# A macaron transformer block on one core: the first feed-forward takes both blocks for each group of weights, and the stages between run in an order written by hand

## The chip, the cores and the metric

The kernel runs on one core of one Trainium2 chip. The metric is the device time of one execution in microseconds. Three runs of the kernel before took 3497.04, 3499.12 and 3503.48 us, so the median is 3499.12. The engines have short names in all that follows: PE (TensorE, matmul), PEld (its weight loads), DVE (VectorE), ACT (ScalarE), POOL (GpSimd) and SP (SyncE, which here only issues DMA transfers). Each engine has its own queue and works through it in order.

## The reference

The input x is 4 batches of 1024 rows of 512 floats. What is computed is a feed-forward, an attention and the same feed-forward again, each added to x:

```
x = x + 0.5 * ffn(layernorm(x))
x = x + attn(layernorm(x))       # 32 heads of 16, 8 of keys and values, rotary positions
x = x + 0.5 * ffn(layernorm(x))
```

The feed-forward's weights are quantised first, which is part of the work: each weight is rounded to bfloat16, and in groups of 64 it becomes -scale, 0 or scale, where scale is the group's mean magnitude (0 where twice the magnitude does not exceed the scale). Then gate and up are two products of x with 2048 columns each, h = silu(gate) * up, h is divided by its root mean square per row, and a last product brings it back to 512 columns. In attention the largest score of each row is subtracted before the exponential, and the sums of the exponentials divide at the end.

## The kernel before

Rows of x are kept in tiles of 128 rows by 512 (`x_b_i`), and a *block* is four of them, 512 rows, so a batch has two blocks and there are eight in all. The hidden 2048 columns are cut into 16 *groups* of 128 (`hc`). Values that need more than one pass of TensorE's fast 32-bit format are split in two (`high` and `low`, `xT` and `xL`), and each product is made with both.

The program is a row of stages. First comes a feed-forward over the two blocks of batch 0 ("0a" in tile names), which also quantises the weights. Then, for each batch, come the *stage between* (`attention_input_output`, L520), a feed-forward over three blocks (some of old batches that are finished, some of coming ones), and the *heads* of that batch. A last stage between and a last feed-forward of two blocks end it.

*The first feed-forward* (L963 to L971, `FeedForward.chunks` at L392). For block 0, `prepare` calls `ternary_weights` (L105) for each group: three loads of 256 KB into `w`, a cast to 16 bits on ACT (L120), a reduction by groups on DVE (L122), the scales spread out on ACT (`wide`, L128), eight DVE instructions of 128x1536 for magnitude, comparison, sign and rounding (L137 to L148), twelve transposes on PE, and three copies back on ACT, of which two, the gate and up weights, are also stored in DRAM (`d_guT`, L158) and widened to 32 bits (L102). The group's products follow: 16 matmuls for gate and up (L289), Silu on ACT (L299), the product h on DVE (L301), its square and the running sum on POOL (L309, L313), high on ACT (L315), low on DVE (L317), and, one group later, eight matmuls of the projection (L329). For block 1 the gate and up weights come back from DRAM, and ten of its groups also turn one tile of the attention weights (`attention_weights`, L164) and store it in `d_w`. In this feed-forward the order of the instructions on each engine is chosen by the framework's planner, from costs and dependencies. The later feed-forwards are in program order (`tc.manual_schedule`, L383).

*The stage between* (L520) normalises eight tiles of the new batch, turns them (L210), multiplies them with the weights of queries, keys and values (L633), adds biases (L647 to L649), rotates (two products on POOL, L659 and L660, a product and a sum on DVE, L661 and L662), turns the result (L671, L672), splits it and stores it in `d_q` and `d_k` (L679, L684). In between it projects the old batch's heads (`put`, L734), adds the result to x (L745 on DVE, L746 on POOL), and normalises the first block of the next feed-forward (`follow`). With `new` absent, in the last one, only the projection and `follow` are left. The planner orders this stage too.

*The heads* go through 128 steps per batch (`run`, L847). A step makes scores (L862), exponentials (L873) and weighted sums (L883) of one part of one of eight key groups, and beside it the row maxima of groups to come. When a group's maxima are complete, they are turned, stored in `d_m` and read back as rows (`mT`, L803 and L816), with transfers issued by POOL. After every second group the sums are fetched back, inverted, stored, and read as `rec`; POOL multiplies `aT` with it (L716):

```
if self.after and n in (self.when + 7, self.when + 12):
    self.after.pop(0)()          # first invert, then multiply
```

`self.when` is the step at which the pair of groups ended (32, 64, 96). The transfers that load a place in the ring of weights, queries and keys (`Places`) are issued by SP when the place is free; in steps 100 and after, these are the weights of the next stage between (`p_in`, `p_out`).

## Time and profile before

| | |
|---|---|
| median of three runs | 3499.12 us |
| profiled execution, its own time | 3501.13 us |
| its span, first to last instruction | 3499.3 us |
| granted PE clock, mean | 0.978 |
| PE, DVE, ACT, POOL busy | 95%, 62%, 51%, 26% |
| first feed-forward, to the last projection of block 1 | 0 to 295.8 us |
| stages between, batches 0 to 3, and the last | 62.6, 87.7, 87.1, 88.7, 49.9 us |
| heads of batches 0 to 3 | 345.7, 340.1, 341.4, 329.2 us |

A line of a group of instructions reads: line in the kernel, engine, operation, output and inputs, their shapes, how many; then the busy time and the mean duration of one in ns; then how long the engine was idle just before them, and what ended that. A line of a timeline begins with the start and the duration in us, and the idle time before it stands in brackets. A line of busy times by stretch has each engine's busy time with the number of its instructions, then the clock granted to PE, the DMA engines' busy share, and GB/s. "SPq" and "POOLq" are transfers issued by that engine.

### The profile page before, as it was taken

Reading aid. Unit: us, or ns where it says so; the run is one execution under the profiler, and the core shown is the slowest. Engines: PE = TensorE matmul, PEld = TensorE weight load, DVE = VectorE, ACT = ScalarE, POOL = GpSimd, SP = SyncE. Lnnn points to the kernel's source line nnn. Section 1 sums busy time; section 2 is a strip of 40 time slices with the busy share of each in tenths; the row PEclk is TensorE's granted clock in tenths of the full one; section 3 lists DMA queues with packets and bytes.
Section 4 is the critical chain, followed back from the end, with each engine's and each line's share of the span. In section 5 each row is a group of like instructions: output and inputs, shape, how many; then the busy total and the mean of one; then the engine's idle time right before and its main releaser. Section 6 shows DMA issues by size and latency. Waiting matters only on the chain. (4 is left out here: it accounts for less than half of the span.)

```text
span 3499.3 us, 57264 instructions
## 1 busy us (share of the span) xinstructions
PE 3321.5 (95%) x22744; PEld 2151.5 (61%) x22744; DVE 2170.9 (62%) x3663; ACT 1769.6 (51%) x2372; POOL 912.0 (26%) x880
## 2 busy tenths in 40 slices
PE   5699999999989999999899999999899999999899
PEld 3577677644448777544467777444487776444587
DVE  8945566677725666677535666777346666775243
ACT  5642333377852333587733333788613334787343
POOL 2344333300014333101123333000133432010144
PEclk9999999999999999999999999999999999999999
DMA  5233322122223133132223222223231221232011
GB/s 183 78 93 102 98 59 76 51 82 89 90 74 107 55 90 100 40 108 94 81 59 101 82 69 64 66 88 103 66 103 57 87 90 56 90 98 71 27 49 55
DMA packets 211115, 282.66 MB, mean 81 GB/s; under 512 B 25760, under 2 KB 155808, under 8 KB 210848
## 3 DMA queue, kind: packets, MB, share of 16 engines
q1 hardware_dynamic: 205728, 276.89, 25.6%
q8 instruction: 179, 2.93, 0.3%
q0 software_dynamic: 5120, 2.11, 0.3%
q14 instruction: 88, 0.72, 0.1%
HBM read 220.20 MB, written 58.72 MB: 80 GB/s over the span
## 5 line engine op out<-in xcount | busy, mean ns | idle before, releaser
L774 DVE TENSOR_REDUCE pm<-sm 128x1 f32<-128x512 f32 x2048 | 1285.1, 685 | 378.6 <-PE sm L765 375.3
L873 ACT ACTIVATE e<-s 128x1024 f32<-128x1024 f32 x1024 | 996.8, 1022 | 345.4 <-PE s L862 342.8
L765 PE MATMUL sm<-p_m,p_m 32*128 32x512 f32 x4096 | 769.8, 440 | 23.6 <-DVE h L301 10.0
L289 PE MATMUL gu<-xT,guT 128*128 128x512 f32 x1792 | 706.1, 394 | 4.9 <-ACT guT L102 4.6
L289 PE MATMUL gu<-xL,guT 128*128 128x512 f32 x1792 | 700.7, 391 | 0.0
L862 PE MATMUL s<-p_s,p_s 32*128 32x512 f32 x4096 | 679.6, 440 | 0.5 <-DMA p_s<-d_k 0.4
L862 PEld LDWEIGHTS s<-p_s,p_s 32*128 32x128 f32 x4096 | 315.7, 186 | 457.6 <-ACT e L873 435.4
L883 PE MATMUL o<-e,vs 128*32 128x512 f32 x4096 | 557.0, 616 | 2.8 <-ACT e L873 2.8
L862 PE MATMUL s<-mT,ones_r 2*128 2x512 f32 x2048 | 415.8, 400 | 25.3 <-DMA mT<-d_m 25.2
L765 PEld LDWEIGHTS sm<-p_m,p_m 32*128 32x128 f32 x4096 | 355.4, 185 | 118.2 <-DVE h L301 66.8
L309 POOL TENSOR_TENSOR sq<-h 128x512 f32<-128x512 f32 x210 | 218.4, 1040 | 704.4 <-DVE h L301 704.1
L289 PEld LDWEIGHTS gu<-xT,guT 128*128 128x128 f32 x1792 | 337.6, 188 | 80.0 <-ACT guT L102 5.5
L289 PEld LDWEIGHTS gu<-xL,guT 128*128 128x128 f32 x1792 | 337.6, 188 | 69.0
L301 DVE TENSOR_TENSOR h<-sg,gu 128x512 f32<-128x512 f32 x224 | 153.9, 687 | 361.2 <-PE gu L289 358.4
L299 ACT ACTIVATE sg<-gu 128x512 f32<-128x512 f32 x224 | 134.2, 599 | 481.4 <-PE gu L289 481.4
L329 PE MATMUL po<-w_pT,high 128*128 128x512 f32 x896 | 372.0, 415 | 0.0
L329 PE MATMUL po<-w_pT,low 128*128 128x512 f32 x896 | 351.6, 392 | 0.1
L315 ACT CAST high<-h 128x512 fp32r<-128x512 f32 x224 | 139.0, 620 | 346.0 <-DVE h L301 341.8
L102 ACT CAST guT<-g 128x512 fp32r<-128x512 bf16 x448 | 274.7, 613 | 15.1 <-DMA g<-d_guT 8.1
L313 POOL TENSOR_TENSOR acc<-acc,sq 128x512 f32<-128x512 f32 x205 | 275.8, 1346 | 16.1
L862 PEld LDWEIGHTS s<-mT,ones_r 2*128 2x128 f32 x2048 | 199.3, 187 | 55.7 <-DMA mT<-d_m 28.3
L329 PEld LDWEIGHTS po<-w_pT,high 128*128 128x128 f32 x896 | 168.9, 189 | 97.5 <-issue 66.0
(134 smaller groups left out, 3032.4 us busy)
## 6 DMA issues: line engine op xcount, KB each, us to landing
g<-d_guT SPq DMA_DIRECT2D x448, 128.0 KB
p_m<-d_k SPq DMA_DIRECT2D x64, 512.0 KB
p_s<-d_k SPq DMA_DIRECT2D x64, 512.0 KB
p_m<-d_q SPq DMA_DIRECT2D x32, 512.0 KB
p_s<-d_q SPq DMA_DIRECT2D x32, 512.0 KB
d_o<-oT SPq DMA_DIRECT2D x64, 256.0 KB
x<-in_L_attn_x_dram SPq DMA_DIRECT2D x32, 256.0 KB
w<-in_L_ffn_w_gate_up_dram SPq DMA_DIRECT2D x32, 256.0 KB
```

The lines of the kernel that those rows point to most:

```text
L102: nc.scalar.copy(w, t)
L289: nc.tensor.matmul(pg, lhsT=self.weights[k, hc][part][:, c, :], rhs=xp[:, c, :], start=(c == 0 and low == 0), stop=(c == DC - 1 and low == 1),
L301: nc.vector.tensor_tensor(h, sg, gu[1], ALU.mult)
L309: nc.gpsimd.tensor_tensor(sq, h, h, ALU.mult)
L313: nc.gpsimd.tensor_tensor(acc, acc, sq, ALU.add)
L315: nc.scalar.copy(high, h)
L329: nc.tensor.matmul(self.pos[k][i], lhsT=h[:, i * P : (i + 1) * P], rhs=w_pT[hc], start=(hc == 0 and n == 0), stop=(hc == HC - 1 and n == 1),)
L765: nc.tensor.matmul(s, lhsT=q[at, i * P : (i + 1) * P], rhs=k[part][at, half * 512 : (half + 1) * 512], start=(part == 0), stop=(part == 1),)
L774: nc.vector.tensor_reduce(pm[:, i, j, half : half + 1], s, AX.X, ALU.max)
L862: nc.tensor.matmul(s[:, e, :], lhsT=k[part][at, keys] if part < 2 else ones_r[at, :], rhs=(q if part < 2 else self.mrows[g])[at, queries], ...
L873: nc.scalar.activation(w, s, AF.Exp, scale=1.0 / HD**0.5)
L883: nc.tensor.matmul(o[j * SLOT : (j + 1) * SLOT, :], lhsT=vs[:, kc, g, :], rhs=es[j // 2][:, j % 2, :], start=(kc == 0), stop=(kc == NT - 1),)
```

## The change

The first feed-forward is a class of its own, `First`. It takes the blocks of batch 0 together: group `i` of the loop quantises ahead (loads of group i+4, cast of i+3, scales and doubled magnitudes of i+2, signs and rounding of i+1), turns the weights of group i, and makes gate and up of block 1 for group i-2 and of block 0 for group i. Block 0 is projected within the loop (group i-2); block 1's hidden values are all kept, and projected after it (`projection`). Twice the magnitude is made by ACT (one activation, Abs with scale 2) instead of two DVE instructions. The weights turned go straight to 32 bits on ACT, and POOL makes the 16-bit copy that is stored. Block 0's low halves are made by POOL; block 1's squares by ACT. The attention weights are turned in groups 5 to 14. The first group is done by thirds of its columns, and only four tiles of x are loaded ahead of the first weights. All is in program order.

The stages between are in program order too, as `input_output` and `output`. The gate weights of the next feed-forward are fetched at their head and widened at their end. In `output` the four tiles of the next block are projected first and normalised together; before, statistics, turns and projections took turns. In the heads the multiplication comes at `self.when + 15`. Memory is laid out anew (x in tagged slots, `vs` in the ring's pool). The mathematics is the same.

The core of the diff:

```diff
+    class First(FeedForward):
+        def groups(self):
...
+            with tc.tile_pool(name="f0a", bufs=1) as wp, tc.tile_pool(name="wstage", bufs=1) as stage:
+                self.wp, self.stage = wp, stage
+                with tc.manual_schedule():
+                    self.begin_groups()
+                    for i in range(HC + 2):
+                        self.group(i)
+                    self.end(0, self.factors(0))
+        def projection(self):
+            with tc.manual_schedule():
+                for c in range(2):
+                    self.split(c)
+                    self.parts[1, c][1]()
+                for c in range(HC):
+                    if c + 2 < HC:
+                        self.split(c + 2)
+                    self.project(1, c, self.parts[1, c][0], [0, 1])
+                    self.project(1, c, self.parts[1, c][0], [2, 3])
+                    if c + 2 < HC:
+                        self.parts[1, c + 2][1]()
+                    if 6 <= c < 10:
+                        load_x(2, c - 6)
+                    if c == HC - 2:
+                        half = self.factors(1)
+                self.end(1, half)
...
+        def double(self, hc, some=ALL):
+            if hc < HC:
+                if hc not in self.twice:
+                    self.twice[hc] = self.sixteen("twice", hc, 2)
+                for a, z in some:
+                    at = slice(a * P, z * P)
+                    nc.scalar.activation(self.twice[hc][:, at], self.wb[hc][:, at], AF.Abs, scale=2.0)
...
+                wide, mask, wb, q = (
+                    t[hc][:, at] for t in (self.wide, self.twice, self.wb, self.q)
+                )
+                nc.vector.tensor_tensor(mask, mask, wide, ALU.is_gt)
+                nc.vector.tensor_scalar(q.bitcast(bits), wb.bitcast(bits), 0x8000, None, ALU.bitwise_and)
+                nc.vector.tensor_tensor(
+                    q.bitcast(bits), q.bitcast(bits), wide.bitcast(bits), ALU.bitwise_or
+                )
+        def quantize(self, hc, some=ALL):
+            for a, z in some if hc < HC else ():
+                at = slice(a * P, z * P)
+                mask, wb, q = (t[hc][:, at] for t in (self.twice, self.wb, self.q))
+                nc.vector.tensor_tensor(q, q, wb, ALU.subtract)
+                nc.vector.tensor_tensor(q, q, wb, ALU.add)
+                nc.vector.tensor_tensor(q, q, mask, ALU.mult)
+        def transpose(self, hc, part):
+            pt = self.ps.tile([P, DC, P], BF16, tag="gu", name=f"pw_{hc}_{part}")
+            for c in range(DC):
+                at = (part * DC + c) * P
+                nc.tensor.transpose(pt[:, c, :], self.q[hc][:, at : at + P], ident16)
+            if part == 2:
+                nc.scalar.copy(w_pT[hc].rearrange("p (c k) -> p c k", k=P), pt)
+                return
+            name = f"guT_{hc}_{part}"
+            w = (widened.tile if part else self.stage.tile)(
+                [P, DC, P], F32R, tag="guT", name=name, bufs=3
+            )
+            nc.scalar.copy(w, pt)
+            w16 = narrow_tile(f"g16_{hc}_{part}")
+            nc.gpsimd.tensor_copy(w16, w.bitcast(F32))
+            nc.sync.dma_start(d_guT[hc, part], w16.rearrange("p c k -> p (c k)"))
+            for k in range(2):
+                self.weights.setdefault((k, hc), []).append(w)
...
+        def halves(self, k, hc, engine):
+            h = self.units[k, hc]
+            high, low = (
+                self.keep.tile([P, 512], F32R, tag=n, name=f"{n}_0a_{k}_{hc}", bufs=self.LAG + 1)
+                for n in ("high", "low")
+            )
+            nc.scalar.copy(high, h)
+            self.parts[k, hc] = (high, low), lambda: engine.tensor_tensor(
+                low, h, high.bitcast(F32), ALU.subtract
+            )
+        def tally(self, k, hc, square):
+            h = self.units.pop((k, hc))
+            if hc == 0:
+                acc = self.keep.tile([P, 512], F32, tag="acc", name=f"acc_0a_{k}", bufs=1)
+                self.accs[k] = [acc]
+                square(acc, h)
+            else:
+                acc = self.accs[k][0]
+                sq = self.keep.tile([P, 512], F32, tag="sq", name=f"sq_0a_{k}_{hc}")
+                square(sq, h)
+                nc.gpsimd.tensor_tensor(acc, acc, sq, ALU.add)
+        def split(self, hc):
+            self.halves(1, hc, nc.vector)
+            self.tally(1, hc, nc.scalar.square)
+        def begin_groups(self):
+            thirds = [((a, a + 4),) for a in (0, 4, 8)]
+            for i in range(4):
+                load_x(0, i)
+            self.load(0)
+            for i in range(4, NT):
+                load_x(0, i)
+            for third in thirds:
+                self.cast(0, third)
+            self.load(1)
+            self.double(0, thirds[0])
+            scales = normal_scales(self.tiles(0), "0a_0")
+            for widen in self.scales(0, thirds[0]):
+                widen()
+            turns = list(self.normalize(0, range(4), self.wp, self.ps, "gu", 4, scales))
+            self.signs(0, thirds[0])
+            self.quantize(0, thirds[0])
+            for turn in turns:
+                turn()
...
+        def group(self, i):
+            self.finish(0, i - 1)
+            if 2 <= i:
+                for some in ([0, 1], [2, 3]):
+                    self.project(0, i - 2, self.parts[0, i - 2][0], some)
+            if 1 <= i <= HC:
+                self.halves(0, i - 1, nc.gpsimd)
+                self.parts[0, i - 1][1]()
+                self.tally(0, i - 1, lambda dst, h: nc.gpsimd.tensor_tensor(dst, h, h, ALU.mult))
+            if 1 <= i < HC:
+                for part in range(3):
+                    self.transpose(i, part)
+            steps = self.scales(i + 2)
+            if i < 2:
+                if i > 0:
+                    self.start(0, i)
+                some = [2 * i, 2 * i + 1]
+                scales = normal_scales(self.tiles(1, some), f"0a_1_{i}")
+                self.signs(i + 1)
+                for turn in self.normalize(1, some, self.wp, self.ps, "gu", 4, scales):
+                    turn()
+            else:
+                self.start(1, i - 2)
+                self.signs(i + 1)
+            if 5 <= i < 15:
+                turn = self.attention_weights(i - 5)
+            self.cast(i + 3)
+            self.load(i + 4)
+            self.double(i + 2)
+            for widen in steps:
+                widen()
+            if i >= 2:
+                self.finish(1, i - 2)
+            if 2 <= i < HC:
+                self.start(0, i)
+            self.quantize(i + 1)
+            if 5 <= i < 15:
+                turn()
+            if 2 <= i < 2 + NT:
+                load_x(1, i - 2)
...
+    def output(old, put, then, wp, ps):
+        for i in range(6):
+            put(i, range(DC - 1))
+        while old.after:
+            old.after.pop(0)()
+        for i in range(4):
+            put(i, range(DC - 1, DC))
+        scales = normal_scales(then.tiles(0), "last")
+        for i in range(4, 6):
+            put(i, range(DC - 1, DC))
+        put(6, range(DC))
+        turns = list(then.normalize(0, range(4), wp, ps, "pt", 4, scales, 2))
+        turns[0]()
+        turns[1]()
+        put(7, range(DC))
+        turns[2]()
+        turns[3]()
+    def input_output(new, old, put, then, wp, ps):
+        turn = None
+        for n in range(NT + 2):
+            if n == 0:
+                new.normalize(0, wp, new.scales(0))
+            if 1 <= n <= NT:
+                new.project(n - 1, ps)
+            if n >= 2:
+                new.rotate(n - 2)
+            scales = new.scales(n + 1) if n + 1 < NT else None
+            after = normal_scales(then.tiles(0, [n - 5]), f"f_{new.b}_{n}") if 5 <= n < 9 else None
+            if n >= 2:
+                new.rotated_sum(n - 2)
+            if scales is not None:
+                new.normalize(n + 1, wp, scales)
+            behind, turn = turn, None
+            if after is not None:
+                (turn,) = then.normalize(0, [n - 5], wp, ps, "pt", 2, after)
+            if behind is not None:
+                behind()
+            if put is not None:
+                for i in {3: (0, 1), 4: (2,), 5: (3,), 8: (4,), 9: (5,)}.get(n, ()):
+                    put(i, range(DC))
+            if n < NT:
+                new.turn_in(n, wp, ps)
+            if n >= 2:
+                new.turn(n - 2, wp, ps)
+            if put is not None and 1 <= n < 3:
+                old.after.pop(0)()
+        places.done(("in", new.b))
+        places.load(("m", new.b, 0))
+        if put is not None:
+            for i in (6, 7):
+                put(i, range(DC))
...
-                if self.after and n in (self.when + 7, self.when + 12):
+                if self.after and n in (self.when + 7, self.when + 15):
```

## The prediction

> **What bounds the kernel now.** The page says TensorE (PE), busy 95%, so I looked for where PE is not busy. First the busy time by stretch, cut at the stage borders that PE's timeline shows: to the first gate matmul, block 0 of the first feed-forward, block 1, the stage between for batch 0, the same for batch 1, and the last one.
>
> ```profile
> PE 3321.5 (95%) x22744; PEld 2151.5 (61%) x22744; DVE 2170.9 (62%) x3663; ACT 1769.6 (51%) x2372; POOL 912.0 (26%) x880
> ```
> ```profile
> core 0: us, PE busy (x) PEld busy (x) DVE busy (x) ACT busy (x) POOL busy (x), PEclk, DMA share, GB/s
> 0.00:34.50 34.50, 5.92 (x28) 4.06 (x28) 25.94 (x50) 12.61 (x14) 4.80 (x14) 1.00 0.80 271
> 34.50:198.00 163.50, 117.57 (x572) 87.70 (x573) 149.38 (x181) 100.38 (x143) 58.38 (x29) 0.93 0.28 88
> 198.00:295.80 97.80, 97.45 (x460) 80.50 (x459) 36.47 (x55) 44.03 (x75) 46.14 (x38) 0.99 0.31 94
> 295.80:358.40 62.60, 55.38 (x280) 47.49 (x279) 44.43 (x97) 11.64 (x26) 22.98 (x24) 0.93 0.45 136
> 1027.60:1115.30 87.70, 81.99 (x412) 71.42 (x409) 46.95 (x96) 13.17 (x29) 32.41 (x30) 0.96 0.36 99
> 3264.50:3314.40 49.90, 35.68 (x149) 29.59 (x146) 13.96 (x28) 2.93 (x5) 13.29 (x12) 0.86 0.12 33
> ```
> Until 198 us PE idles 74 us while VectorE (DVE), which quantises, is busy 91% of block 0; block 1 then has PE busy throughout and DVE 37%. The batch stages idle 6 to 7 us each, the last one 14.
>
> Next the groups of instructions of the first 200 us, and one of the page:
> ```profile
> L309 POOL TENSOR_TENSOR sq_0a<-h_0a 128x512 f32<-128x512 f32 x15 | 33.0, 2199 | 97.5 <-DVE h_0a L301 97.4
> L122 DVE TENSOR_REDUCE wmean<-wb 128x24 f32<-128x1536 bf16 x16 | 27.9, 1742 | 1.2 <-ACT wb L120 1.2
> L313 POOL TENSOR_TENSOR acc_0a<-acc_0a,sq_0a 128x512 f32<-128x512 f32 x15 | 26.8, 1785 | 1.2
> L120 ACT CAST wb<-w 128x1536 bf16<-128x1536 f32 x16 | 23.6, 1473 | 8.2 <-DVE wq L147 7.0 <-DMA w<-in_L_ffn_w_proj_dram 1.2
> L144 DVE TENSOR_TENSOR wq<-wq,wide 128x1536 uint16<-128x1536 uint16 x16 | 18.1, 1134 | 0.3
> ```
> ```profile
> L309 POOL TENSOR_TENSOR sq<-h 128x512 f32<-128x512 f32 x210 | 218.4, 1040 | 704.4 <-DVE h L301 704.1
> ```
> The same square takes GpSimd (POOL) 1.04 us, and 2.20 beside the quantising. Last, three timelines (POOL, DVE, PE) near the end of the heads of batch 0, and the chain that ended last:
> ```profile
> 977.63 2.34 POOL L716 TENSOR_TENSOR aT<-aT,rec 128x1024 f32<-128x1024 f32 x1 [53.15 <-DMA rec<-d_r]
> 979.91 0.58 POOL L803 DMA_DIRECT2D d_m<-mrow  x1
> ```
> ```profile
> 968.51 0.28 DVE L801 CAST mrow<-pmT 64x128 fp32r<-64x128 f32 x1 [1.90 <-PE pmT L799]
> ```
> ```profile
> 984.16 1.27 PE L862 MATMUL s<-mT,ones_r 2*128 2x512 f32 x2 [7.76 <-DMA mT<-d_m]
> ```
> ```profile
> 2610.29 17.23 DMA p_m<-d_k
> ...
> 3275.52 6.75 DMA rec<-d_r
> 3282.34 2.34 POOL aT L716
> ...
> 3325.34 1.81 PE po L329 x8
> 3327.16 3.63 PE gu L289 x16
> ```
> The maxima were ready at 968.79, but their store stood behind the multiply on POOL's queue, which waited for rec until 977.6. PE lost 7.76 us there, and 8.78 and 8.67 at 1733 and 2482; at 3221 the chain shows 1.84.
>
> **The change, part by part.** Profiled execution: 3501.13 us, span 3499.3; median 3499.12, so 2 above it.
>
> *Before the third group.* w_0 now follows 4 x loads, not 20, so PE's first gate matmul comes near 17 instead of 34.5. DVE sets what follows: up to group 2's transposes it quantises three groups, 7.0 us each once starts overlap (1.74 reduce, 0.17 scale, is_gt 0.95, sign bits 0.55, or 0.95, three of 0.95, less about 0.08 of overlap each), normalises and splits 8 x tiles (0.67+0.18+0.55+0.68, 1.8 spaced), and 1.3 more: 21+14.5+1.3 = 37. From its first x at 3.4 that is 40; I add 8 for hand-overs to ACT and POOL in the thirds (0.5 to 1.0 each). Group 2 begins at 48 (42 to 54).
>
> *Groups 2 to 15.* PE: 8 projections 1.81, 12 transposes 0.84, two passes of 16 gate and up matmuls 7.26: 9.9, and 0.4 in the ten groups that turn attention weights. DVE: 7.0 and two products of 0.69, 8.3; |2w| (0.78+0.55) and low (0.99) leave it, waits behind POOL (wscale 0.51 on average, 0.17 alone) add about 1. ACT: cast 1.47, wide 1.47, Abs about 1.47 by L120's shape, three weight copies 0.6, two Silu 0.6, high 0.62: 8.0, with the attention copy 8.6. So none passes PE by its sum, but the queues' order does: SP's stores of d_guT now wait for POOL's two casts to 16 bits, and the load of wa stands behind them, with its transposes at the end of the same group on PE. POOL begins when high is there (1.6): low 1.3, square 2.0, add 1.5 (between 1.04 or 1.28 alone and the loaded rows), two casts 0.9 each, which no row shows: bounded by 0.5 (half of vs's memset, 0.95 for twice the elements) and 2.2 (the loaded square), nearer the lower as they have one input. That ends at 8.2; 0.6 for the issue and 2.6 to land (x_0_0: issued 0.75, read 3.39) give 11.4, transposes 0.4: 11.8 a group. Queued behind it: w's load, which then lands 4 us before its cast, and on PE the next projections. Ten at 11.8 and four at 10.2: 159 (143 if PE alone binds, 189 at 13.5).
>
> Abs beside Silu: no row has it. ACT_TABLE_LOAD is 1.283, and copies and Silu alternate in block 0 with none between; a bound is 0 to two per group, which the 11.8 mostly covers. I take 0. The Trainium skill ("ScalarE: Activation LUTs", Table sets) says that abs is filler in every set, which also makes 0; no run shows it yet.
>
> *Groups 16, 17 and the end of block 0.* Two of 5.44: 10.9. Then factors, power 1.03 on POOL, four updates 2.73, and block 1's first low 0.68 stand on PE's path: 5.4.
>
> *Block 1's projections.* 16 x 1.81 = 29, with 1 for the squares, which go through one buffer (ACT 0.6, POOL add 1.3, so near 2.0 a step against 1.81, with a lead of two): 30 (29 to 35). Its last projection ends at 48+159+10.9+5.4+30 = 253 instead of 295.8: 42 saved (12 to 57).
>
> *Stage between, batch 0.* Before: 62.6. PE's sum is 50.9 (eight tiles of pq 3.45, pkv 1.73 and 0.97 of transposes, four turns of 0.43). In fixed order the updates of block 1 (1.5 past PE's end), statistics, power, rows and turn stand ahead of the first projection: 5.2, where before the turn was made inside the feed-forward, and p_in, now loaded under the projections, cost 2.46. At the end the last rotation (adds 0.9, POOL 2.0, sum 0.8, lows ahead of it 1.2) stays bare. 64.5: 2 lost (-3 to +6).
>
> *Stages for batches 1 to 3.* PE needs 78.6 (the 50.9 and eight pa of 3.45); with start 1.5, bare copies and the last rotation about 84 against 87.7. But the first maxima need p_m, which lands 23 us after the last turn (17.23 of it the transfer). Two projections follow that turn now, not three: 3.45 of this cover goes, and where PE waited 0.7 to 0.9 it will wait near 4. So 0.6 each, 2 in all (-8 to +8).
>
> *Heads.* The multiply moves three steps (7.5 us) back, from step 108 to 111, the maxima's store and load (steps 109, 110) now precede it. Both pieces, 1.8 and up to 4 to land, run within the burst of p_in loads (rec took 8.8): mT is there near 976 to 979, wanted at 976. 6.3 of each 8.4 goes, and 1.5 at 3221: 20 saved (12 to 27). Its rec transfer is issued later too, but SP, in order, came to it at 968.7 behind the p_in loads anyway, and nothing waits for that product before the heads end. The other two multiplies of a batch meet no want of mT.
>
> *Costed at nothing.* The gate weights' fetches at the head of each batch stage: six issues of some 0.4 on SP, idle there, behind the last den transfer; if it were not, den would be late and with it aT. x loads moved into the groups (256 KB each in eight): DMA's share is 0.28 in block 0, and they are last on SP in their group. vs's memset, 0.95 on POOL, lies beside the end of block 0.
>
> *Last stage.* The aT multiply ends at 3284.7 as now. Before, 29.7 us follow it, PE taking statistics, turns and whole projections in turn. After: four last pieces 3.5, the last add on POOL 3291.6, statistics 0.9, power 1.0, rows, turns, with put(7) between them: gate at 3302. 12 saved (8 to 14).
>
> Sum: 42-2+2+20+12 = 74, so 3501-74 = 3427.
>
> The Trainium skill ("GPSIMD Engine Reference", Engine selection) speaks against part of this: it puts two-input elementwise work on VectorE, as GpSimd is about twice as slow. The trace agrees (square 1.04 to 2.20, DVE's low 0.99). By that rule low stays on DVE, the chain on POOL is 1.3 shorter and the ten groups save 13 us, 3414; by my rows DVE has the room and it costs the 13.
>
> **The rivals.**
> 1. *PE binds the groups*: POOL keeps near its unloaded 1.04 and 1.28, so wa is in time. 143 for 159: 3411. For it: DVE idles within a group; against it: the loaded rows.
> 2. *The queues bind harder*: POOL at its loaded rows throughout, 13.5 a group. 189: 3457. For it: 2.20 and 1.79; against it: DVE's share falls to 70%.
> 3. *The heads keep their stall*, since d_m and mT go through the burst anyway: 3447. For it: DMA share 0.9 there; against it: 8 KB pieces.
> 4. *Slower: the casts on POOL.* At c us each the ten groups take 10.0+2c and the other four 6.2+2c once POOL binds, 28c-34 above my 159; the 74 are spent at c = 3.9, beyond it the kernel is slower, 3519 at 4.5. For it: no such cast is in the trace; against it: 3.9 is 1.8 times POOL's longest 512-element row, the loaded 2.20.
>
> **How the numbers follow.** Mine 0.52, rivals 0.16, 0.15, 0.11 and 0.05; 0.01 that all gains end within 7 us, 0.2%, which is about what a measurement here can tell from no change. Faster 0.94, same 0.01, slower 0.05. The range goes from rival 1 with 27 in the heads and 14 in the last stage, 3402, to rival 2 with 8 lost in the batch stages instead of 2 saved, 3467; outside lie rival 4 and combinations of the ends, under 2 in 10.
>
> **What would show it.** Right: last projection of block 1 near 253; PE in groups waiting for wa's DMA; no wait over 3 us on mT; p_m's wait near 4 after each batch stage; the last stage near 37 us. Wrong: a period above 13, table loads in each group, or a heads stall that stays.

## The result, and the profile after

The changed kernel takes 3518.01 us (median of four runs) beside 3501.27 for the kernel before on the same chip: a ratio of 1.0048, 95% interval 1.0031 to 1.0066. It is slower by half a per cent, where 3427 was predicted. The profiled execution took 3512.53 us with a span of 3510.8, 11.4 more than that of before (3510.75 against 3499.34). The page gives it the same busy share as before, and PE's clock is 0.973 on the mean, before 0.978:

```profile
PE 3329.0 (95%) x22736; PEld 2154.4 (61%) x22736; DVE 2169.1 (62%) x3626; ACT 1762.8 (50%) x2346; POOL 931.6 (27%) x908
```

So the page as a whole tells nothing; the stages do. Busy times of the changed kernel by stretch: the first two groups, the loop of groups, block 1's projections, the stages between of batches 0 and 1, and the last one.

```profile
core 0: us, PE busy (x) PEld busy (x) DVE busy (x) ACT busy (x) POOL busy (x), PEclk, DMA share, GB/s
18.30:61.90 43.60, 21.72 (x76) 15.28 (x76) 30.38 (x51) 22.37 (x25) 7.27 (x8) 0.59 0.23 73
61.90:235.10 173.20, 156.43 (x816) 125.91 (x816) 143.05 (x139) 104.70 (x139) 94.07 (x77) 0.99 0.40 122
235.10:268.50 33.40, 32.02 (x136) 25.81 (x136) 19.54 (x23) 15.32 (x26) 19.46 (x16) 0.95 0.28 104
268.50:339.60 71.10, 56.41 (x280) 47.34 (x280) 49.01 (x109) 13.04 (x30) 25.87 (x27) 0.94 0.28 78
1005.00:1102.10 97.10, 83.86 (x409) 71.47 (x409) 49.11 (x105) 14.53 (x32) 35.34 (x33) 0.96 0.31 85
3277.70:3325.50 47.80, 34.47 (x149) 28.85 (x145) 14.32 (x26) 3.41 (x7) 13.68 (x10) 0.86 0.14 35
```

The stage of batch 1 is 97.1 us where it was 87.7, with PE idle 13 us in it instead of 6. Cut the same way on PE's timeline, the kernels of this study that bear on these stages stand side by side (us; the names are those of the experiments below):

| | before | after | b15 | a_old | a_rec | a_cover | a_both | a_rot | a_best |
|---|---|---|---|---|---|---|---|---|---|
| first feed-forward | 295.8 | 268.5 | 296.4 | 270.6 | 271.8 | 268.2 | 269.9 | 270.8 | 251.9 |
| stage between, batch 0 | 62.6 | 71.1 | 61.7 | 61.3 | 69.9 | 71.1 | 69.7 | 68.5 | 60.0 |
| the same, batches 1 to 3, sum | 263.5 | 290.0 | 262.5 | 262.7 | 268.6 | 293.4 | 283.7 | 264.1 | 265.5 |
| feed-forwards behind these three, sum | 963.2 | 988.0 | 972.3 | 961.1 | 988.1 | 977.1 | 964.4 | 972.4 | 963.2 |
| heads, sum of four | 1356.3 | 1335.3 | 1330.9 | 1331.5 | 1337.5 | 1335.3 | 1336.4 | 1331.4 | 1333.8 |
| last stage | 49.6 | 47.7 | 50.5 | 51.3 | 48.5 | 48.0 | 48.3 | 47.8 | 40.5 |

From before to after: 27.3 and 21.0 gained in the first feed-forward and the heads, 1.9 in the last stage; 8.5, 26.5 and 24.8 lost in the stages between and in the feed-forwards that follow them. The feed-forward of batch 0 adds 1.8. PE's waits, in total, times and longest, name the places. Before:

```profile
PE s L862 <- DMA mT<-d_m: 25.2, 3, 8.8
PE pa L734 <- POOL aT L716: 4.4, 1, 4.4
PE sm L765 <- DMA p_m<-d_k: 2.4, 3, 0.9
```

After:

```profile
PE pa L1008 <- POOL aT L990: 23.4, 4, 6.2
PE sm L1037 <- ACT sg L221: 15.5, 3, 5.8
PE pxn L136 <- DVE xn L125: 7.0, 2, 6.7
PE s L1134 <- DMA mT<-d_m: 6.7, 4, 2.8
```

The wait for `mT` went, as meant. In its place stand 23 us for `aT`, the product with `rec` (18 of them in the three stages, 5 in the last one, where before had 4.4), and 15.5 in front of the first maxima (`sm`). For the latter the trace names ACT's Silu, which was long done; it is the transfer of `p_m`, as experiment a_cover shows.

### The profile page after: what moved, and what is told of

It is laid out like the page before. It is cut to its first block, busy times and chain, and to the rows that moved or that the text cites. A ratio compares the mean times of both kernels' runs of the same rounds, so it can differ in the third digit from the quotient of the medians.

```text
span 3510.8 us, 57082 instructions
## 1 busy us (share of the span) xinstructions
PE 3329.0 (95%) x22736; PEld 2154.4 (61%) x22736; DVE 2169.1 (62%) x3626; ACT 1762.8 (50%) x2346; POOL 931.6 (27%) x908
## 4 chain that ended last, share of the span: by engine, by line
PE 79%; DVE 6%; DMA 5%; issue 5%; POOL 3%; ACT 2%; SPq 0%; POOLq 0%; DVEq 0%; ACTq 0%
PE gu L211 21%; PE s L1134 16%; PE o L1155 13%; PE po L251 11%; PE sm L1037 7%; PE pq L908 3%; PE pa L1008 2%; DMA g<-d_guT 2%; DVE pm L1046 1%; PE pkv L908 1%; PE gu_0a L532 1%; DVE x L286 1%; DMA p_s<-d_k 1%; PE pxn L136 1%; DMA rec<-d_r 1%
## 5 line engine op out<-in xcount | busy, mean ns | idle before, releaser
L1037 PE MATMUL sm<-p_m,p_m 32*128 32x512 f32 x4096 | 773.6, 441 | 36.3 <-ACT sg L221 15.5
```

Of the source, the lines that this page charges most:

```text
L1037: nc.tensor.matmul(s, lhsT=q[at, i * P : (i + 1) * P], rhs=k[part][at, half * 512 : (half + 1) * 512], start=(part == 0), stop=(part == 1),)
```

## The experiments

Each ratio is to the kernel before, run on the same chip. "Against after" is the difference of the ratios times 3500 us; one such difference is uncertain by about 8 us, so small effects are read in the traces too.

**Which part gains and which loses.** b15 is the kernel before with one edit:

```diff
-                if self.after and n in (self.when + 7, self.when + 12):
+                if self.after and n in (self.when + 7, self.when + 15):
```

> The kernel before with the heads part of the change alone: the multiply moves from step 7+5 to step 7+8 behind the end of a pair of head groups, all else as before. Theory (the heads part is a gain by itself, and the batch stages lose time for reasons of their own): PE's waits on mT near 984, 1733 and 2482 us (7.8, 8.8, 8.7) shrink to 2 or less, the three stages behind the heads stay at 87 to 89 us, and the kernel comes to 3477 to 3483, ratio to before 0.993 to 0.995. Rival A (the burst of loads holds mT anyway; the shorter heads in the changed kernel came from their later start): waits on mT stay above 5, 3496 to 3502. Rival B (the later multiply is what makes the stages behind the heads longer): the heads save 20 but each stage loses 6 to 9, 3497 to 3508.

Measured: 3481.56 us, ratio 0.9949 (0.9934 to 0.9964). PE's waits on `mT` went from 25.2 to 6.0:

```profile
PE s L862 <- DMA mT<-d_m: 6.0, 3, 3.3
```

The three stages keep their 87 to 88 us. The heads part is a gain of 18 us by itself, and the later multiply is not what made the stages longer. In the table's column the heads gain 25 us and the feed-forwards behind them lose 9: in batches 1 and 3 PE waits 1.95 and 2.95 us for the first maxima, with 3.4 and 6.8 us of half clock. Why is open; a_old, which has the later multiply too, shows no such loss.

a_old is the changed kernel with `project_in`, `project_out` and `attention_input_output` of the kernel before, left to the planner:

```diff
-        ) as ps, tc.manual_schedule():
+        ) as ps:
...
-                input_output(new, old, put, then, wp, ps)
+                steps = new.project_in(wp, ps)
+                for n, step in enumerate(steps):
+                    step()
...
```

> The changed kernel with the stage between heads and feed-forward, the last one too, written and ordered as before; the first feed-forward by groups and the later multiply stay. Theory (all that was lost was lost by the fixed order of this stage): the batch stages come back from 96 to 97 to 87 to 89, batch 0's from 71 to 63 to 65, the feed-forwards behind them from 329 to 330 to 321, last stage 50: 62 saved and 2 given back, 3454 to 3464, ratio to before 0.987 to 0.990. Rival (the losses come with the earlier start, the later multiply or a slower clock and not with the order): stages and feed-forwards keep at least half of what they lost, 3488 to 3515.

Measured: 3451.1, ratio 0.9864 (0.9847 to 0.988), 64 below the changed kernel. The table shows where: 27 us in the three stages, 27 in the feed-forwards behind them, 10 in batch 0. The stages between as rewritten are the whole loss; the rest of the change gains 1.4%. This run puts back the planner's order and with it some buffers and the place of the gate weights' fetches, so by itself it doesn't say what in the rewriting costs; the next runs ask that.

**What in that order costs.** SP's queue behind the heads of batch 0 (start, duration), with POOL's multiply, after:

```profile
1010.73 0.33 SPq L985 DMA_DIRECT2D d_r<-den  x1
1019.90 0.37 SPq L963 DMA_DIRECT2D d_q<-qh  x1
1020.32 0.99 SPq L968 DMA_DIRECT2D d_k<-qh  x2
...
1023.04 0.59 SPq L989 DMA_DIRECT2D rec<-d_r  x1
1029.86 2.34 POOL L990 TENSOR_TENSOR aT<-aT,rec 128x1024 f32<-128x1024 f32 x1 [14.07 <-DMA rec<-d_r]
```

Before:

```profile
1033.09 0.44 SPq L711 DMA_DIRECT2D d_r<-den  x1
1038.93 0.60 SPq L715 DMA_DIRECT2D rec<-d_r  x1
1041.52 0.37 SPq L679 DMA_DIRECT2D d_q<-qh  x1
1045.38 2.34 POOL L716 TENSOR_TENSOR aT<-aT,rec 128x1024 f32<-128x1024 f32 x1 [7.91 <-DMA rec<-d_r]
```

Before, `rec` was issued 5.8 us after the store of the inverted sums and ahead of the first tile's stores; after, the stores of `d_q` and `d_k` stand ahead of it on SP's queue, they wait for that tile's turn, and `rec` is issued 12.3 us after. In the code the cause is one line: the second `old.after.pop(0)()` comes behind `new.turn(0)`. In the kernel before the statements stand in the same order, behind the step that turns tile 0, but there the planner set the order on each queue. a_rec moves the transfer, not the multiply:

```diff
+            if put is not None and n == 2:
+                old.fetch_rec()
             if 1 <= n <= NT:
                 new.project(n - 1, ps)
...
```

`fetch_rec` issues `rec<-d_r`.

> The changed kernel with one transfer issued earlier: rec, of the last multiply, is put on SP's queue at the beginning of step 2 of the stage, ahead of the six stores of d_q and d_k of the first turn; the multiply itself stays where it is. Theory (SP's order makes rec late: issued 18 us behind the heads' end, before it was 12): rec is issued 4 to 6 us sooner, PE's wait of 6.1 for aT goes below 2, and the three batch stages lose 5 to 9 each with the half-speed clock behind the wait: 3491 to 3503. Rival (rec then waits for d_r's store or in the burst of p_in, t1 and gate loads, or the multiply for POOL's rotations): the wait stays above 4 and the time at 3511 to 3520.

Measured: 3494.66, ratio 0.9986 (0.9972 to 1.0), 22 against after. PE's waits for `aT` fall to 5.8, of which 4.8 are the last stage's:

```profile
PE pa L1016 <- POOL aT L996: 5.8, 3, 4.8
```

The three stages become 21 us shorter: each had waited some 6.1 us, and in batch 1 the 6.8 us at half clock that began in this wait are gone as well. Of the edits tried alone in these stages, this one is worth most.

a_cover changes only what covers `p_m`:

```diff
-                for i in {3: (0, 1), 4: (2,), 5: (3,), 8: (4,), 9: (5,)}.get(n, ()):
+                for i in {3: (0, 1), 4: (2,), 5: (3,), 9: (4,)}.get(n, ()):
...
-            for i in (6, 7):
+            for i in (5, 6, 7):
```

> The changed kernel with three whole projections behind the last turn of a batch stage, as before, where the change leaves two: projection 5 moves from step 9 to the end. Theory (p_m's transfer starts with the last turn's store, so what stands behind that turn is its only cover; the uncovered wait of 4.9 also halves the clock for what follows): the wait goes below 2, the feed-forwards of batches 1 to 3 lose 5 to 8 each, 3495 to 3505. Rival A (the clock's drop belongs to the first maxima and not to the wait): 2 to 3.5 each, 3508 to 3513. Rival B (the turn comes no sooner, since the last rotation binds and projection 5 covered that): the stage becomes longer by what the feed-forward gains, 3514 to 3520.

Measured: 3506.46, ratio 1.0023 (1.0009 to 1.0036), 9 against after: between the two. The wait fell from 4.90 to 1.57, but the feed-forwards gained only 11 us in all. The granted clock tells why. Stretches around the first maxima of batch 1, PE alone (busy, clock, DMA share, GB/s), after:

```profile
1114.60:1119.00 4.40, 0.05 (x2) 1.00 0.37 103
1119.00:1125.60 6.60, 6.05 (x16) 0.50 0.36 114
1125.60:1131.60 6.00, 6.00 (x32) 0.98 0.29 90
```

a_cover:

```profile
1116.60:1118.50 1.90, 0.33 (x3) 1.00 0.26 94
1118.50:1125.40 6.90, 6.62 (x19) 0.51 0.39 116
1125.40:1131.40 6.00, 6.00 (x32) 1.00 0.34 89
```

In both, PE then works 6.1 and 6.6 us at half its clock, which loses 3.0 to 3.3 us whether the wait was 4.9 or 1.6. In batches 2 and 3 of a_cover the waits are 1.20 and 0.64 us in the one and 1.18 and 0.28 us in the other; the half clock lasts 3.4 us in the one and is absent in the other. To see whether the drop goes with the wait, a_both puts four projections (4 to 7) behind the last turn, and takes a_rec's edit too:

```diff
-                for i in {3: (0, 1), 4: (2,), 5: (3,), 8: (4,), 9: (5,)}.get(n, ()):
+                for i in {3: (0, 1), 4: (2,), 5: (3,)}.get(n, ()):
...
-            for i in (6, 7):
+            for i in (4, 5, 6, 7):
```

> The changed kernel with rec's transfer issued before the first turn's stores and with four whole projections (4 to 7) behind the last turn of a batch stage. Theory (what the fixed order lost in batches 1 to 3 is these two things, and the half-speed clock comes with any wait on p_m above about 1.5 us): stages at 88 to 91, the wait on p_m below 0.6 with no drop of the clock behind it, feed-forwards of batches 1 to 3 at 320 to 322, 3466 to 3476; what then lies above the 3451 of the version with the old stages is batch 0's stage and the start. Rival A (the drop of the clock belongs to the first maxima and not to the wait): feed-forwards at 324 to 327, 3480 to 3488. Rival B (the projection taken out of step 8 covered the rotations): stages 93 or more, 3480 to 3490.

Measured: 3480.29, ratio 0.9949 (0.9931 to 0.9967). The feed-forwards are back at 320.9 to 321.9, with no wait and no drop:

```profile
1112.00:1118.00 6.00, 6.00 (x32) 1.00 0.44 101
1118.00:1124.00 6.00, 6.00 (x32) 1.00 0.37 116
```

So the clock goes with the wait, and rival A falls. But the stages take 94 to 95 us, 15 more in the three than with a_rec alone: rival B. The moved projections had also covered the last rotation, for which PE now waits 4.33 us in each stage instead of 1.80, with 6.8 us at half clock around it.

That rotation has a cause of its own. In batch 0 the last turn on PE begins 7.0 us after the last projection's end in the changed kernel (330.18 to 337.17), 4.0 with the old order: VectorE first works off `xL` and the low halves of the tile before, and only then the last tile's additions. a_rot issues the additions one step earlier, with a_rec's edit and three projections at the end:

```diff
-            if n >= 2:
-                new.rotate(n - 2)
...
             if n < NT:
                 new.turn_in(n, wp, ps)
+            if 1 <= n <= NT:
+                new.rotate(n - 1)
             if n >= 2:
                 new.turn(n - 2, wp, ps)
```

> The changed kernel with rec's transfer early, three whole projections behind the last turn, and each tile's three additions and its rotation issued one step earlier, ahead of the turn of the tile before, so that VectorE's low halves of that turn no longer stand ahead of them. Theory (in the fixed order the last tile's additions stand behind low halves and xL on VectorE: the last turn comes 7.0 us after the last projection, with the old order 4.0, and this leaves a wait that must be covered too): the last turn comes 4 to 5 us after the last projection, batch 0's stage loses 3 to 4, the stages of batches 1 to 3 take 86 to 90, the feed-forwards behind them 320 to 323, 3455 to 3468. Rival (the low halves, now behind the additions, make the stores late or hold the turns): stages 93 or more, 3475 to 3490.

Measured: 3472.18, ratio 0.9945 (0.9925 to 0.9965). That lies between theory and rival. The stages of batches 1 to 3 are at 87.5 to 89.0, as expected, and PE's wait for the last rotation is gone in them. But batch 0's loses only 1 to 2 from the other edits' 70, and its last turn still comes 6.2 us after the last projection; and the feed-forwards of batches 2 and 3 take 326 and 325 us, not 320 to 323. In batch 2 PE waits 1.43 and 0.65 us for the maxima, in batch 3 0.44 and 0.29, each with 3.4 us at half clock behind it. The mechanism is there in the three stages; in batch 0 it is worth 0.8 us, not 2 to 3.

**The first feed-forward.** a_wa moves the load of attention weights to the head of its group:

```diff
         def group(self, i):
+            if 5 <= i < 15:
+                turn = self.attention_weights(i - 5)
             self.finish(0, i - 1)
...
-            if 5 <= i < 15:
-                turn = self.attention_weights(i - 5)
             self.cast(i + 3)
```

> The changed kernel with each load of attention weights issued at the beginning of its group, ahead of the group's two stores of d_guT on SP's queue. Theory (SP's order makes wa late: the ten groups that turn attention weights wait 0.9 to 3.0 us on it, 10.2 in all): these waits go, the ten groups run at 10.6 to 10.8 like the plain ones instead of 11.6 and 15.0 for the first, and the kernel comes 8 to 10 lower, 3507 to 3511. Rival (POOL's chain or DVE is next in these groups and takes the wait's place): 0 to 3 lower, 3514 to 3520.

Measured: 3506.19, ratio 1.002 (1.0005 to 1.0035), 10 against after. In after, PE had waited for `wa` 10.8 us in all; here the ten groups run at 10.6 us without a wait for it, and the last projection ends at 258.4. SP's order made the 11.6.

a_low makes block 0's low halves on VectorE:

```diff
-                self.halves(0, i - 1, nc.gpsimd)
+                self.halves(0, i - 1, nc.vector)
```

> The changed kernel with low of block 0's units made on VectorE (as before, 0.99 us) and not on GpSimd. Theory of the prediction (the chain on POOL, low, square, add, two casts, sets when the stores of d_guT and behind them wa's load are issued; VectorE has room): the chain is 1.3 shorter, the waits on wa of 0.9 to 1.2 go, groups with attention weights at 10.6 to 10.8, 5 to 10 lower, 3508 to 3513. Rival (VectorE is full too: reduce 1.74, is_gt 0.95, signs 1.40 and 1.93, three steps of 0.95 to 1.3, two products of 0.68 and the scale come to 10.3 of the plain group's 10.6, so another 0.99 on it makes it the bound): plain groups at 11.0 to 11.6, 0 to 10 slower, 3518 to 3528.

Measured: 3505.0, ratio 1.0018 (1.0002 to 1.0033), 10 against after; groups from the third on take 10.4, and the last projection ends at 258.0. VectorE has one more instruction in each group and is less busy. Plain groups and attention groups by stretch (columns as in the first such fence), after:

```profile
62.00:104.00 42.00, 38.16 (x200) 30.72 (x200) 41.45 (x40) 29.98 (x37) 25.68 (x20) 1.00 0.36 116
117.00:175.00 58.00, 52.44 (x281) 41.71 (x279) 55.81 (x53) 39.35 (x50) 32.63 (x25) 1.00 0.51 150
```

a_low:

```profile
62.00:104.00 42.00, 40.23 (x212) 32.69 (x212) 38.70 (x45) 31.18 (x38) 15.10 (x16) 1.00 0.45 141
113.00:174.00 61.00, 61.00 (x329) 49.58 (x328) 56.09 (x65) 46.01 (x60) 22.62 (x24) 1.00 0.56 164
```

The groups of instructions show it in the sign steps, L470 and L471. In the changed kernel POOL makes `low` first, so that its square, its sum and its first cast fall beside these two steps (only in one of the eleven groups is it `low` itself). One group, after:

```profile
95.09 1.30 POOL L571 TENSOR_TENSOR low_0a<-h_0a,high_0a 128x512 fp32r<-128x512 f32 x1 [4.13 <-ACT high_0a L570]
96.34 1.83 POOL L643 TENSOR_TENSOR sq_0a<-h_0a 128x512 f32<-128x512 f32 x1
97.20 1.39 DVE L470 TENSOR_SCALAR wq<-wb 128x1536 uint16<-128x1536 uint16 x1
98.26 1.49 POOL L586 TENSOR_TENSOR acc_0a<-acc_0a,sq_0a 128x512 f32<-128x512 f32 x1
98.63 1.93 DVE L471 TENSOR_TENSOR wq<-wq,wide 128x1536 uint16<-128x1536 uint16 x1
```

In a_low POOL's work ends sooner and it is idle beside them. All eleven and twelve groups, after:

```profile
L471 DVE TENSOR_TENSOR wq<-wq,wide 128x1536 uint16<-128x1536 uint16 x11 | 21.0, 1909 | 0.4
L470 DVE TENSOR_SCALAR wq<-wb 128x1536 uint16<-128x1536 uint16 x11 | 14.2, 1291 | 3.8 <-PE pw L489 3.8
```

a_low:

```profile
L471 DVE TENSOR_TENSOR wq<-wq,wide 128x1536 uint16<-128x1536 uint16 x12 | 11.5, 959 | 0.4
L470 DVE TENSOR_SCALAR wq<-wb 128x1536 uint16<-128x1536 uint16 x12 | 6.6, 548 | 0.0
L571 DVE TENSOR_TENSOR low_0a<-h_0a,high_0a 128x512 fp32r<-128x512 f32 x12 | 12.5, 1042 | 8.2 <-ACT high_0a L570 8.2
```

Taking `low` to POOL freed 1.04 us on VectorE and cost it 1.69 in these two lines alone. In the attention groups PE, 61.0 busy of 61.0, is now the bound; PE's waits for `wa` are down from 10.8 us to 0.6.

a_start reorders ScalarE in the first groups, which moves two loads up, and normalises both rows of a group ahead of their turns:

```diff
             self.double(0, thirds[1])
+            self.cast(1)
+            self.load(2)
             steps[0]()
             self.transpose(0, 0)
+            self.double(0, thirds[2])
...
             self.transpose(0, 1)
-            self.cast(1)
-            self.load(2)
+            self.cast(2)
+            self.load(3)
...
-                for turn in self.normalize(1, some, self.wp, self.ps, "gu", 4, scales):
+                for turn in list(self.normalize(1, some, self.wp, self.ps, "gu", 4, scales)):
```

> The changed kernel with the casts of groups 1 and 2 moved up on ScalarE into its idle time between the thirds, the loads of groups 2 and 3 behind them, and both rows of a group normalised ahead of their two turns. Theory (in the first 62 us VectorE is busy 43 and waits 15, on transfers and on ScalarE's order: 3.4 for group 2's cast, 2.4 for a third's scales, 6.6 in four waits for xT): group 2's transposes begin at 53 to 57 us instead of 61.9, and the kernel comes 5 to 9 lower, 3509 to 3513. Rival (PE's half-speed clock in this stretch, 0.70 on the mean, sets the turns and what waits for them): not before 60, 3515 to 3520.

Measured: 3508.22, ratio 1.0034 (1.0018 to 1.0049), 5 against after. In its trace group 2's transposes begin at 53.5 instead of 61.9, and the last projection ends at 260.6. VectorE's reduction of group 2, after and then a_start:

```profile
31.80 1.75 DVE L441 TENSOR_REDUCE wmean<-wb 128x24 f32<-128x1536 bf16 x1 [3.36 <-ACT wb L420]
```
```profile
27.64 1.75 DVE L441 TENSOR_REDUCE wmean<-wb 128x24 f32<-128x1536 bf16 x1
```

**The last stage.** VectorE in the changed kernel:

```profile
3302.74 0.69 DVE L1017 TENSOR_TENSOR ao<-pa,bo 128x512 f32<-128x512 f32 x1 [1.38 <-POOL x L1018]
3304.81 0.69 DVE L1017 TENSOR_TENSOR ao<-pa,bo 128x512 f32<-128x512 f32 x1 [1.38 <-POOL x L1018]
...
3315.43 0.69 DVE L1017 TENSOR_TENSOR ao<-pa,bo 128x512 f32<-128x512 f32 x1 [1.37 <-POOL x L1018]
3316.03 2.41 DVE L125 TENSOR_SCALAR xn<-x,mv_last,rstd_last 128x512 f32<-128x512 f32 x3
```

`ao` has one buffer, so each addition on VectorE waits for POOL to take the row before, and the normalised rows, whose power was ready at 3312.1, stand behind three additions. a_last makes two edits at once, and which of them gains how much is not shown:

```diff
         scales = normal_scales(then.tiles(0), "last")
+        turns = list(then.normalize(0, range(4), wp, ps, "pt", 4, scales, 2))
         for i in range(4, 6):
             put(i, range(DC - 1, DC))
         put(6, range(DC))
-        turns = list(then.normalize(0, range(4), wp, ps, "pt", 4, scales, 2))
...
-                    ao = wp.tile([P, D], F32, tag="ao", name=f"ao_{b}_{i}")
+                    ao = wp.tile([P, D], F32, tag="ao", name=f"ao_{b}_{i}", bufs=2 if bufs > 2 else 1)
```

> The changed kernel with two buffers for ao in the last stage and the four rows normalised ahead of the last projections' additions. Theory (with one buffer DVE's addition waits for POOL's addition of the row before, 2.07 us a row, and the normalised rows stand behind three of these on DVE): the wait of 6.75 on xn falls below 2 and the last stage takes 38 to 41 us instead of 47.7, 3508 to 3511. Rival (POOL's additions bind by themselves, and the power on POOL behind them): the stage keeps 45 to 48, 3515 to 3520.

Measured: 3512.19, ratio 1.004 (1.0025 to 1.0055), 3 against after and within its uncertainty; the stage itself fell from 47.7 to 39.8 in the trace, with the rows at 3310.28 and this wait on PE:

```profile
3310.88 1.18 PE L136 MATMUL pxn<-ident,xn 128*128 128x128 f32 x8 [0.86 <-DVE xn L125]
```

**Together.** a_best is a_old with the edits of a_wa and a_start, and the last stage of a_last by hand.

> The first feed-forward by groups with the earlier wa loads and the reordered start, the later multiply, the stages between as in the kernel before, and the last stage in the fixed order with two ao buffers and the rows ahead. Theory (the gains lie in different stages and add up): from the 3451 of the version with the old stages, 9 off for wa, 7 for the start and 9 for the last stage: 3422 to 3434, ratio to before 0.979 to 0.982. Rival (they cover one another, a shorter group waiting elsewhere): 3440 to 3451.

Measured: 3419.52, ratio 0.9783 (0.9767 to 0.98): 2.2% faster than the kernel before. The gains lie in different stages and add up.

a_best2 keeps the fixed order, with all its mends: a_rot with the edits of a_wa, a_start and a_last, and low on VectorE from group 3 on.

> All edits of the fixed order together: rec early, three projections behind the last turn, additions one step earlier, wa's load at the beginning of its group, the reordered start, low on VectorE from group 3 on, two ao buffers and the rows ahead in the last stage. Theory (each is worth in it what it is worth alone): from 3462 for the first three, 10 off for wa, 8 for the start, 2 for low, 8 for the last stage: 3428 to 3440, at most 20 above the version with the planned stages, 3419.5. Rival (the fixed order, once mended, is no worse than the planned one): 3410 to 3422.

Measured: 3443.55, ratio 0.985 (0.9829 to 0.9871). It ends its first feed-forward 4 us sooner than a_best (247.9), but its stage of batch 0 takes 69.6 against 60.0, and its feed-forwards of batches 1 to 3 take 977 against 963: PE waits 0.6, 1.95 and 1.92 us for the first maxima there, with 3.4, 6.8 and 3.4 us at half clock behind it. The mended order is still the worse one. Why the hand order of batch 0 stays 9 us behind the planned one after these mends is not settled by a run. The traces show where the time lies: PE idles 5.3 us more there (11.5 against 6.2; three waits of 0.9 to 1.4 for `xL` and one of 1.15 for the gate weights, which the planned order doesn't have), and it is busy 3.5 us more, at a clock of 0.92 against 0.97.

## Why the prediction was wrong

*Groups 2 to 15, 16 and 17, the end of block 0*: right. From group 2's transposes to block 1's first projection it is 173.2, predicted 159 + 10.9 + 5.4 = 175. The attention groups took 11.6 (predicted 11.8) for the reason given, as a_wa shows. POOL's cast, which no row had, is 0.95 against 0.9. Abs beside Silu brought no table load into the groups: the two on ACT's timeline up to 66 us stand at 0.74 and 18.27, none later. This agrees with the Trainium skill ("ScalarE: Activation LUTs", Table sets), as drawn on in the prediction. The plain groups took 10.6, not 10.2, and not by PE's sum: VectorE is busy 41.45 of 42.00 us in them, where the prediction put its work at 8.3 a group and about 1 of waits. It missed that what VectorE does beside POOL's longer chain takes up to twice as long (a_low).

*Before the third group*: wrong by 14. The step was "I add 8 for hand-overs". VectorE is busy 43.05 us up to 62, not 37 (and the 7.0 a group in that sum is 6.6 by the rows given with it), and idle about 15 after its first x. These waits come from ACT's order (a cast behind a third's copies) and from rows and turns alternating; a_start takes 8 of them. With block 1's projections at 33.4 instead of 30 (half clock for 3.4 us behind a 4.1 us wait that precedes them, 0.95 over them), 27 was saved and not 42.

*Stage between, batch 0*: wrong by 7. The sum was 64.5, though the terms written out for it (50.9, 5.2, 4.9) make 61.0; measured 71.1. The chain behind the last projection is 3 us longer than in the old order, and PE's waits for `xL` between the tiles (4.2 us) and for the gate weights at the end (1.15) were not counted.

*Stages for batches 1 to 3*: here the prediction failed. "So 0.6 each" were 26.5 lost in the stages and 24.8 behind them. First, the sum took PE's instructions, the start and the rotation, and no step of it asked when `rec` is issued; yet the diff shows it behind the first turn's stores on SP (a_rec: 22 us). Second, p_m's wait was priced near 4 and took 4.8 to 5.8, but it was priced only as a wait; the half clock behind it costs another 2 to 3 (a_cover, a_both). Third, the two covers compete: what stands behind the last turn is taken from the last rotation (a_both).

*Heads*: right, 20 predicted and 21.0 measured, and by the mechanism named: PE's waits on `mT` fell from 25.2 to 6.7; b15 alone gains 18.

*Last stage*: 12 predicted, 1.9 measured. The step counted PE's pieces and POOL's last addition, and missed that one `ao` buffer ties VectorE to POOL row by row (2.07 us each); with two buffers and the rows ahead the stage is 8 shorter.

*The weighed rule*: the prediction set the rule that two-input elementwise work belongs on VectorE against its own rows, 13 us apart. a_low measures 10 (uncertain by 8): the rule was worth about its price. The rows it was set against, by which VectorE had the room, were those of a VectorE without POOL's longer chain beside it. The rivals 1 to 4 are not what happened; the kernel is slower, but by none of them (rival 4 needed a cast of 3.9 us).

The sum against the profile: -27.3 + 8.5 + 26.5 + 24.8 - 21.0 - 1.9 + 1.8 = 11.4.

## What to carry to other kernels

Where an order is written out by hand, go through every queue that issues transfers and ask for each transfer what stands ahead of it and what that waits for; a sum of PE's work doesn't show it. A wait of PE can cost more than itself: those of 1.2 us or more for the first maxima cost the wait plus 1.7 to 3.6 us, the work lost at half clock behind it. Not every wait does: three of 1.4 to 1.8 us in the stage of batch 1 (after) brought no half clock. A step taken off a full engine may slow that engine from its new place, so look at the durations of what will run beside it.

## What was not expected of the hardware

*The clock after short waits.* Around PE's waits for the first maxima the granted clock fell to half for none, one, two or three steps of 3.4 us. None: waits of 0.50 (a_old), 0.69 to 0.93 (before), 0.78 (a_rot, batch 1) and 1.18 (a_cover, batch 3). One: 0.44 (a_rot, batch 3), 0.56 and 1.92 (a_best2), 1.20 (a_cover, batch 2), 1.95 (b15, batch 1). Two: 1.57 (a_cover, batch 1), 1.95 (a_best2, batch 2), 4.90 (after). Three: 5.84 (a_rec, batch 2) and 6.58 (a_low, batch 1), where a part of them lies in the wait itself. What PE works at half clock behind the wait is 3.4 to 7.2 us, so the price is 1.7 to 3.6 us of work, and below 2 us the wait's length alone does not decide it. (Behind some of these waits stands a second one, of 0.3 us and twice 0.65.) The wait of 1.95 us, in b15 and then in a_best2 (PE alone, as above):

```profile
1120.30:1123.70 3.40, 3.40 (x9) 0.50 0.34 127
```
```profile
1825.70:1832.50 6.80, 6.64 (x17) 0.50 0.37 107
```

In each run's trace the half-clock stretches begin on one grid of 3.41 us, from the first to the last, whatever PE waits for; where a wait falls on this grid may be what decides, but no run tests it. The Trainium skill ("TensorE: Matmul & The Clock Gate", Part 1) describes two states, full and half, decided in windows of about 3.4 us that run freely, and has the clock fall after an idle one; the states and the step of 3.4 us agree, but here waits far shorter than a window were enough.

*POOL slows VectorE.* With POOL's square, running sum and cast beside them, VectorE's sign steps took 1.91 and 1.29 us, with POOL idle 0.96 and 0.55 (after and a_low); POOL's own square took 1.64 and 1.04, its cast 0.97 and 0.61. The Trainium skill ("GPSIMD Engine Reference", Key points) says that the two share memory interfaces and contend when VectorE has two inputs or runs in a two-port performance mode; the runs agree for the step with two inputs, don't show the mode of the other, and put a factor of 2.0 and 2.4 on these two lines.
